# A 3x3 convolution as seven products of up to 128 rows from tiles of shifted channel blocks, and smaller tiles for data that comes back from DRAM

## The chip, the cores and the metric

The program runs on one core of a Trainium2 chip. The metric is the device time of one execution in microseconds, the median of several runs. A profile of one further execution goes with it; its times are in microseconds (us) from the start of the span.

## The reference

The input is 32 images of 56 x 56 positions and 96 channels, float32. Two layers follow one another:

```python
# layer 0, each image
h  = layernorm(x) over channels * ln_w + ln_b
x1 = (h @ w_in + b_in)[..., :192]            # the second half of w_in is not used
y  = conv3x3(x1, conv_w, 'SAME') + conv_b    # 192 -> 96 channels
x  = x + silu(y)
# layer 1, on the 3136 positions of an image
t  = x
h  = relu(bn1(layernorm(t) @ w1.T))          # 96 -> 192
X  = fft(h, axis=positions, norm='ortho')
xr = relu(X.real*rd - X.imag*idg + rb);  xi = relu(X.imag*rd + X.real*idg + ib)
t  = t + bn2(real(ifft(xr + 1j*xi)) @ w2.T)  # 192 -> 96
t  = t + qffn(layernorm(t))                  # 96 -> 384 -> 96, values rounded to 8-bit floats
```

## The kernel before

The two linear steps of layer 0 are folded at the start into one 3x3 convolution of 96 normalised channels plus a row of ones for the biases (`weff`, 97 rows, 9 taps). A Fourier transform of 3136 = 112 x 28 points is made of two stages of matmuls with tables.

One image is a tile `t` of 112 partitions x 28 x 96: partition p holds positions 28p to 28p+27. Work goes in seven groups of four columns j (`G4`, `NG`), in the spectrum in seven groups of four frequency pairs (`PG`, `NS`). These are the steps of an image b, with their engines and lines:

- `image`: the normalised input of group g is transposed on TensorE (L258, tile `tp_im`) and copied by VectorE (DVE) into `img` (L265), a zero-padded picture of 97 x 58 x 58, channels on partitions.
- `conv` (L273): nine products, one per tap, each reading `img` shifted by (dy, dx), into a PSUM tile `cv` of 96 x 448. ScalarE (ACT) takes it out with Silu (L275, tile `s`), TensorE transposes it back (L281) and DVE adds it to `t` (L283).
- `layernorm` (L241 to L248), on DVE, ACT and GpSimd (POOL), three times an image: `a` of the next input, `b` after the convolution, `c` after the attention part.
- `channels` and `transform_a` (L288 to L303): transposes, product with `w1`, Relu, first transform stage; the result `u` goes to DRAM as `da`, one DMA per group.
- `spectrum` (L305 to L369): `da` is loaded back into the tile `at` by seven DMAs (L312), into one large buffer. `forward(g, i)` multiplies with the table `fb_sb` (L320, tile `px`), and ACT, DVE and POOL form the rectified spectrum (L330 to L339). `inverse(g)` multiplies with `w2` (L347, `pg`), copies to `gw` on ACT (L349), multiplies with `ib_sb` (L352, `pe`), copies to `es` on DVE (L354), and sends `es` to DRAM as `de` (L355). Between the groups, `between(g)` makes `image` group g of the next image.
- `transform_out`: `de` comes back as `y` by seven DMAs (L368); the last transform stage `py` (L374) is added to `t` (L376), and LayerNorm `c` follows.
- `ffn_in`, `ffn_out` (L381 to L405): the FFN of image b runs interleaved with the convolution of image b+1, group by group.

All these DMAs are issued from one queue, SyncE's (SP). ACT's queue issues three loads at the start and nothing later. The order of instructions on each engine is fixed before the program runs, by a planner that takes the source's order as priority and lets ready work of later steps go ahead; so the transposes of `image` stand ahead of the first `px`, and the convolution of the next image begins before `py`. On the chip each engine then works strictly in that order.

Buffers named below: PSUM tags with two buffers each are `tp` (transposes), `a` (`cv`, `pf`, `pa`), `b` (`pg`, `pe`, `po`), `c` (`ph`, `px`, `py`). In SBUF, `es` has three buffers (pool `w3`), and `y` two, each for a whole image.

Of the kernel before, what the change touches and what calls it, by code (L numbers as in the profile page):

```python
# [32 lines left out]
F32 = mybir.dt.float32  # L36
F16 = mybir.dt.float16
F8 = mybir.dt.float8e5
AF = mybir.ActivationFunctionType
# [3 lines left out]
C = 96  # L43
# [5 lines left out]
PG = 4  # L49
NS = NP // PG  # L50
H = 192
FF = 384
G4 = 4
NG = N2 // G4
EPS = 1e-5
# [11 lines left out]
def first(p):  # L67

    return 2 * (2 * N2 * p + min(p, PG))
# [3 lines left out]
def hybrid_kernel(ctx: ExitStack, tc: tile.TileContext, x, par, w_in, conv_w, w1, w2, fw1, fb1, fw2, fb2, fa, fb, ib, ia, out):  # L73
# [19 lines left out]
    nc.sync.dma_start(par_sb, par)  # L93
    convb = par_sb[:, CONV_B : CONV_B + 1]

    weff = const.tile([C + 1, 9, C], F32, name="weff")
    w1a = const.tile([C + 1, H], F32, name="w1a")
    w2a = const.tile([C, 2, C], F32, name="w2a")
    w1q = const.tile([C, FF], F8, name="w1q")
# [2 lines left out]
    b2q = const.tile([N1, G4, C], F16, name="b2q")  # L102


    img = const.tile([C + 1, HW + 2, HW + 2], F32, name="img")
    n2ts = [const.tile([C + 1, G4, N1], F32, name=f"n2t{i}") for i in range(3)]
    ys = [const.tile([113, N2, C], F32, name=f"y{i}") for i in range(2)]
    scal = const.tile([C, 3, 2], F32, name="scal")

    tpool = ctx.enter_context(tc.tile_pool(name="tpool", bufs=2))  # L110

# [7 lines left out]
    with tc.tile_pool(name="setup", bufs=1) as sp, tc.tile_pool(  # L119
# [12 lines left out]
        for g in range(2):  # L132
            ps = spp.tile([128, 512], F32, tag="ps", name=f"ps_wt{g}")
            nc.tensor.matmul(ps[:C, : C + 1], win[:, g * C : (g + 1) * C], diag, start=True, stop=True)
            nc.vector.tensor_copy(wt[:, g, :], ps[:C, : C + 1])
            nc.vector.tensor_tensor(
                wt[:, g, C : C + 1], wt[:, g, C : C + 1], par_sb[:, B_IN + g : B_IN + g + 1], ALU.add
            )
        for k in range(9):
            ps = spp.tile([128, 512], F32, tag="ps", name=f"ps_we{k}")  # L140
            for g in range(2):
                nc.tensor.matmul(ps[: C + 1, :C], wt[:, g, :], cw[:, g, k, :], start=(g == 0), stop=(g == 1))
            nc.vector.tensor_copy(weff[:, k, :], ps[: C + 1, :C])

        def bn_fold(scale, bias, at, n):

# [30 lines left out]
            nc.vector.tensor_copy(w2a[:, g, :], ps[:C, :C])  # L177
        ps = spp.tile([128, 512], F32, tag="ps", name="ps_o2")
        nc.tensor.transpose(ps[:1, :C], o2, ident[:C, :C])
        row = sp.tile([1, N2, C], F32, name="row")  # L180
        for i in range(N2):
            nc.vector.tensor_copy(row[:, i, :], ps[:1, :C])
        for y in ys:
            nc.sync.dma_start(y[112:113], row)
# [28 lines left out]
            nc.vector.tensor_copy(b2q[:, i, :], b28)  # L213

        nc.gpsimd.memset(img, 0.0)
        nc.gpsimd.memset(img[C : C + 1, 1 : HW + 1, 1 : HW + 1], 1.0)
        for n2t in n2ts:
            nc.gpsimd.memset(n2t[C : C + 1], 1.0)
        nc.sync.dma_start(fb_sb, fb)
        nc.scalar.dma_start(ib_sb, ib)  # L220


    big = ctx.enter_context(tc.tile_pool(name="big", bufs=1))
    xnp = ctx.enter_context(tc.tile_pool(name="xnp", bufs=2))
    work = ctx.enter_context(tc.tile_pool(name="work", bufs=2))
    w3 = ctx.enter_context(tc.tile_pool(name="w3", bufs=3))
# [31 lines left out]
            nc.tensor.transpose(ps[:, j, :], xn[:, g * G4 + j, :], ident[:N1, :N1])  # L258
        return ps

    inside = img[:C, 1 : HW + 1, 1 : HW + 1].rearrange("c r (h j) -> c j r h", h=2)

    def image(xn, b, g):
        ps = to_channels(xn, g, f"im{b}")
        nc.vector.tensor_copy(inside[:, g * G4 : (g + 1) * G4], ps.rearrange("c j (r h) -> c j r h", h=2))  # L265

    def conv(b, g):

        ps = psum.tile([C, N1, G4], F32, tag="a", name=f"cv_{b}_{g}")
        for k in range(9):  # L270
            dy, dx = divmod(k, 3)
            seen = img[:, dy : dy + HW, dx : dx + HW].rearrange("c r (h j) -> c r h j", h=2)
            nc.tensor.matmul(ps, weff[:, k, :], seen[:, :, :, g * G4 : (g + 1) * G4], start=(k == 0), stop=(k == 8))  # L273
        s = work.tile([C, G4, N1], F32, tag="s", name=f"s_{b}_{g}")
        nc.scalar.activation(s, ps.rearrange("c p j -> c j p"), AF.Silu, bias=convb)  # L275
        return s

    def conv_add(s, t, b, g):
        pt = psum.tile([N1, G4, C], F32, tag="tp", name=f"st_{b}_{g}")
        for j in range(G4):  # L280
            nc.tensor.transpose(pt[:, j, :], s[:, j, :], ident[:C, :C])  # L281
        tg = t[:, g * G4 : (g + 1) * G4, :]
        nc.vector.tensor_tensor(tg, pt, tg, ALU.add)  # L283

# [20 lines left out]
    def spectrum(da, b, between):  # L305


        de = dram.tile([NP, 112, C], F32, tag="de", name=f"de_{b}")
        at = big.tile([112, NP, H], F32, tag="at", name=f"at_{b}")
        rows = da.rearrange("n (k p) c -> (n k) p c", p=NP)  # L310
        for g in range(NS):
            nc.sync.dma_start(at[:, g * PG : (g + 1) * PG, :], rows[:, g * PG : (g + 1) * PG, :])  # L312
        gt = {}

        def forward(g, i):
            w = width(g * PG)
            px = psum.tile([C, PG, 2, w], F32, tag="c", name=f"px_{b}_{g}_{i}")
            for j in range(PG):
                p = g * PG + j
                nc.tensor.matmul(  # L320
                    px[:, j], at[:, p, i * C : (i + 1) * C], fb_sb[:, first(p) : first(p + 1)], start=True, stop=True
                )
            if i == 0:
                gt[g] = w3.tile([C, 2, PG, 2, w], F32, tag="gt", name=f"gt_{b}_{g}")
# [16 lines left out]
        def inverse(g):  # L341
            k = 2 * width(g * PG)
            pg = psum.tile([k, PG, C], F32, tag="b", name=f"pg_{b}_{g}")
            for j in range(PG):
                for i in range(2):
                    lhs = gt[g][:, i, j].rearrange("c r k -> c (r k)")
                    nc.tensor.matmul(pg[:, j, :], lhs, w2a[:, i, :], start=(i == 0), stop=(i == 1))  # L347
            gw = work.tile([k, PG, C], F32, tag="gw", name=f"gw_{b}_{g}")
            nc.scalar.copy(gw, pg)  # L349
            pe = psum.tile([112, PG, C], F32, tag="b", name=f"pe_{b}_{g}")  # L350
            for j in range(PG):
                nc.tensor.matmul(pe[:, j, :], ib_sb[:k, g * PG + j, :], gw[:, j, :], start=True, stop=True)  # L352
            es = w3.tile([112, PG, C], F32, tag="es", name=f"es_{b}_{g}")
            nc.vector.tensor_copy(es, pe)  # L354
            nc.sync.dma_start(de[g * PG : (g + 1) * PG].rearrange("p m c -> m p c"), es)  # L355
            del gt[g]

        for g in range(NS + 1):
            if g < NS:
                forward(g, 0)  # L360
                forward(g, 1)
            between(g)
            if g >= 1:
                inverse(g - 1)
        yt = ys[b % 2]
        rows = de.rearrange("p (k n) c -> (p k) n c", n=N2)
        for g in range(NG):
            nc.sync.dma_start(yt[:112, g * G4 : (g + 1) * G4, :], rows[:, g * G4 : (g + 1) * G4, :])  # L368
        return yt  # L369

    def transform_out(yt, t, b, g):

        py = psum.tile([N1, G4, C], F32, tag="c", name=f"py_{b}_{g}")
        nc.tensor.matmul(py, ia_sb, yt[:, g * G4 : (g + 1) * G4, :], start=True, stop=True)  # L374
        tg = t[:, g * G4 : (g + 1) * G4, :]
        nc.vector.tensor_tensor(tg, py, tg, ALU.add)  # L376

# [32 lines left out]
    layernorm(t_next, xa, "a0")  # L410
    for g in range(NG):
        image(xa, 0, g)
    before = None
    for b in range(nb + 1):
        if b < nb:
# [31 lines left out]
            layernorm(t_next, xa, f"a{b + 1}")  # L447

        def between(g):
            if more and g < NG:  # L450
                image(xa, b + 1, g)

        yt = spectrum(da, b, between)
        xc = norm_tile(f"c{b}")
        for g in range(NG):
            transform_out(yt, t, b, g)
            layernorm(t, xc, f"c{b}", ended(g))
        before = xc, t, b

# [95 lines left out]
```

## Time and profile before

| quantity | value |
|---|---|
| median of three runs | 5408.46 us (5400.78 to 5417.65) |
| profiled execution | 5414.79 us outside, span 5413.0 us |
| granted clock of TensorE, mean | 0.89 |
| busy share of TensorE matmuls, DVE, ACT, POOL | 85%, 57%, 36%, 44% |
| `cv` products (L273) | 4032 instructions, 1794.5 us busy |
| DMA bytes, mean rate | 316.72 MB, 59 GB/s |

A float32 product is two instructions in the profile. Matmuls overlap in their pipeline, so the mean duration of one (595 ns for `cv`) is longer than the distance from one start to the next. In the lists of groups and of instructions in time, a line gives source line, engine, operation, output <- inputs, and in brackets the time for which the engine was idle before it and what ended that.

### The profile page before, as it was taken

The page shows a single profiled execution, that of the slowest core. Times are in us where ns is not written, and L with a number is a line of the kernel's source. Part 1 is how long each engine was busy: PE and PEld are TensorE (multiplying, and loading weights), DVE is VectorE, ACT ScalarE, POOL GpSimd, SP SyncE. Part 2 cuts the span into 40 slices and gives each one's busy share as a digit, 9 for nine tenths or more (in the row PEclk, how much of TensorE's full clock was granted, in tenths as well). Part 3 has the DMA queues.
Part 4 walks back from the last instruction along what each step waited for, and adds up shares of the span by engine and source line. Part 5 has one row for each costly group of instructions (what it writes and reads, how often), then busy time and mean ns, then how long its engine had stood idle before and what let it go on. Part 6 is the DMA issues. An engine that isn't in the chain of part 4 may idle for free. (4 is left out here: it accounts for less than half of the span.)

```text
span 5413.0 us, 65386 instructions
## 1 busy us (share of the span) xinstructions
PE 4589.3 (85%) x23123; PEld 2942.3 (54%) x23123; DVE 3073.5 (57%) x6540; ACT 1945.4 (36%) x3970; POOL 2379.5 (44%) x2062
## 2 busy tenths in 40 slices
PE   6888888888888888988888888889888898888886
PEld 3555555555455554555554555545555455555555
DVE  3555555555555555556555555555555556555555
ACT  1333333333333343333433333433334333333333
POOL 3443544444444444444444444444444444434443
PEclk9988898888988889988989888889888898888987
DMA  2122211222202222112222022221222211222112
GB/s 52 52 72 72 57 54 34 72 72 58 66 22 71 72 61 66 48 43 72 72 57 62 26 72 72 59 67 29 62 72 61 65 43 48 72 69 58 52 36 72
DMA packets 277376, 316.72 MB, mean 59 GB/s; under 512 B 118808, under 2 KB 244568, under 8 KB 269656
## 3 DMA queue, kind: packets, MB, share of 16 engines
q1 hardware_dynamic: 275170, 310.44, 20.4%
q8 instruction: 184, 3.01, 0.2%
q10 hardware_dynamic: 1880, 2.09, 0.1%
q14 instruction: 142, 1.16, 0.1%
HBM read 158.31 MB, written 154.14 MB: 58 GB/s over the span
## 5 line engine op out<-in xcount | busy, mean ns | idle before, releaser
L273 PE MATMUL cv<-img,weff 97*96 97x448 f32 x4032 | 1794.5, 595 | 4.6 <-ACT h L387 2.5
L273 PEld LDWEIGHTS cv<-img,weff 97*96 97x96 f32 x4032 | 664.9, 170 | 952.6 <-issue 903.3
L337 POOL TENSOR_SCALAR sv<-sv 96x224 f32<-96x224 f32 (+1 forms) x448 | 428.7, 957 | 890.6 <-DVE sv L335 890.6
L320 PE MATMUL px<-fb_sb,at 112*96 112x112 f32 (+1 forms) x3584 | 568.7, 309 | 84.9 <-issue 51.2
L347 PE MATMUL pg<-w2a,gt 96*112 96x96 f32 (+1 forms) x3584 | 523.5, 299 | 67.1 <-DVE gt L339 64.8
L320 PEld LDWEIGHTS px<-fb_sb,at 112*96 112x96 f32 x3584 | 487.6, 203 | 117.3 <-issue 89.8
L347 PEld LDWEIGHTS pg<-w2a,gt 96*112 96x112 f32 (+1 forms) x3584 | 473.2, 211 | 98.4 <-DVE gt L339 97.5
L275 ACT ACTIVATE s<-cv,par_sb 96x448 f32<-96x448 f32 x224 | 140.4, 627 | 1031.8 <-PE cv L273 1031.8
L330 ACT ACTIVATE av<-px,par_sb 96x224 f32<-96x224 f32 (+1 forms) x448 | 198.2, 442 | 808.7 <-PE px L320 729.6
L405 POOL TENSOR_TENSOR t<-t,y 112x384 f32<-112x384 f32 x224 | 212.8, 950 | 569.1 <-DVE y L403 569.1
L258 PE MATMUL tp_im<-ident,xn_a 112*96 112x112 f32 x896 | 183.9, 372 | 322.2 <-POOL xn_a L248 277.7
L389 DVE TENSOR_SCALAR h<-h,b1q 128x448 f16<-128x448 f16 x672 | 289.9, 454 | 273.6 <-ACT h L387 267.5
L243 POOL TENSOR_TENSOR xn_c<-t,mu_c 112x768 f32<-112x768 f32 (+1 forms) x128 | 167.4, 1308 | 590.6 <-DVE mu_c L242 587.2
L243 POOL TENSOR_TENSOR xn_a<-t,mu_a 112x768 f32<-112x768 f32 (+1 forms) x128 | 165.9, 1307 | 495.1 <-DVE mu_a L242 375.9
L387 ACT CAST h<-pf 128x448 f16<-128x448 f32 x672 | 344.1, 532 | 67.9 <-PE pf L385 65.7
L288 DVE COPY n2t<-tp_n 96x448 f32<-96x448 f32 x224 | 138.4, 618 | 380.9 <-PE tp_n L258 380.9
L301 PE MATMUL pa<-h,fa_sb 112*112 112x384 f32 x896 | 348.6, 510 | 2.4 <-ACT h L299 2.4
L381 DVE CAST n3t<-tp_n 96x448 fp8e5<-96x448 f32 x224 | 137.1, 613 | 372.9 <-PE tp_n L258 372.9
L297 PE MATMUL ph<-w1a,n2t 97*112 97x192 f32 x1792 | 341.1, 327 | 0.0
L258 PEld LDWEIGHTS tp_im<-ident,xn_a 112*96 112x96 f32 x896 | 137.0, 182 | 374.4 <-POOL xn_a L248 362.2
L247 POOL TENSOR_TENSOR var_b<-var_b,mhalf 112x8 f32<-112x8 f32 (+1 forms) x128 | 209.6, 1637 | 217.3 <-DVE var_b L246 215.0
L352 PE MATMUL pe<-gw,ib_sb 112*112 112x96 f32 (+1 forms) x1792 | 266.4, 302 | 42.0 <-ACT gw L349 41.5
(105 smaller groups left out, 7858.8 us busy)
## 6 DMA issues: line engine op xcount, KB each, us to landing
da<-u SPq DMA_DIRECT2D x224, 336.0 KB, 3.2
at<-da SPq DMA_DIRECT2D x224, 336.0 KB, 6.3
t<-in_x SPq DMA_DIRECT2D x32, 1176.0 KB, 7.7
de<-es SPq DMA_DIRECT2D x224, 168.0 KB, 2.3
y<-de SPq DMA_DIRECT2D x224, 168.0 KB, 3.3
out<-t SPq DMA_DIRECT2D x32, 1176.0 KB, 5.9
ib_sb<-in_ib ACTq DMA_DIRECT2D x1, 1396.5 KB
fb_sb<-in_fb SPq DMA_DIRECT2D x1, 1375.5 KB
```

What stands on the lines that cost most here:

```text
L243: nc.gpsimd.tensor_tensor(xc, t[:, j0:j1, :], mu.unsqueeze(2).to_broadcast([N1, n, C]), ALU.subtract)
L258: nc.tensor.transpose(ps[:, j, :], xn[:, g * G4 + j, :], ident[:N1, :N1])
L273: nc.tensor.matmul(ps, weff[:, k, :], seen[:, :, :, g * G4 : (g + 1) * G4], start=(k == 0), stop=(k == 8))
L297: nc.tensor.matmul(ph[:, j, :], n2t[:, 2 * j2 + j, :], w1a, start=True, stop=True)
L301: nc.tensor.matmul(pa, fa_sb, h, start=True, stop=True)
L320: nc.tensor.matmul(px[:, j], at[:, p, i * C : (i + 1) * C], fb_sb[:, first(p) : first(p + 1)], start=True, stop=True)
L337: nc.gpsimd.tensor_scalar(sv[:, 1], sv[:, 1], 0.0, -1.0, ALU.max, ALU.mult)
L347: nc.tensor.matmul(pg[:, j, :], lhs, w2a[:, i, :], start=(i == 0), stop=(i == 1))
L352: nc.tensor.matmul(pe[:, j, :], ib_sb[:k, g * PG + j, :], gw[:, j, :], start=True, stop=True)
L387: nc.scalar.copy(h1, pf)
L389: nc.vector.tensor_scalar(h2, h1, b1q[:, k : k + 1], 0.0, ALU.add, ALU.max)
L405: nc.gpsimd.tensor_tensor(tg, tg, y2, ALU.add)
```

## The change

- The convolution reads three tiles instead of `img`: `ta` and `tb` of 128 partitions and `tcc` of 105, each 56 x 58 positions. `ta` and `tb` hold four 32-channel blocks of the picture, each shifted by its own dx; the shift dy is made when reading, so each serves three products. `tcc` holds the last block (channels 64 to 95 at dx = 2) at three shifts dy, and nine rows of ones (one per tap, for the bias), and serves one product. That is seven products instead of nine.
- The three tiles are built once an image by `pack`: eleven DMAs of 32 partitions x 12,992 bytes from SBUF to SBUF, issued from ACT's queue. `pack` stands after `forward(4)` of the spectrum; to have the picture ready by then, `between` makes two groups of `image` at a time.
- The picture is stored with its two axes exchanged, so that the 56 rows r are contiguous: the DVE copy of `image` writes runs of 56, and the products read runs of 56 (before: runs of 4).
- The weights are arranged into seven tiles `wp` by 20 small DMAs at the start, and the rows of ones are put into `tcc` by nine.
- To make room: `at` becomes three buffers of one group each, loaded three groups ahead; `y` becomes four buffers of one group, loaded inside `transform_out`; `es` has two buffers instead of three (pool `work`).

```diff
-    weff = const.tile([C + 1, 9, C], F32, name="weff")
+    wp = const.tile([128, 7, C], F32, name="wp")
...
-    img = const.tile([C + 1, HW + 2, HW + 2], F32, name="img")
+    img = const.tile([C, P58 + 1, P58], F32, name="img")
+    ta = const.tile([128, HW, P58], F32, name="ta")
+    tb = const.tile([128, HW, P58], F32, name="tb")
+    tcc = const.tile([C + 9, HW, P58], F32, name="tcc")
-    ys = [const.tile([113, N2, C], F32, name=f"y{i}") for i in range(2)]
+    ys = [const.tile([113, G4, C], F32, name=f"y{i}") for i in range(4)]
...
+        for i, blocks in enumerate((BLOCKS_A, BLOCKS_B)):
+            for j, (c, dx) in enumerate(blocks):
+                nc.sync.dma_start(wp[32 * j : 32 * j + 32, 3 * i : 3 * i + 3, :], taps[32 * c : 32 * c + 32, dx])
+        for dy in range(3):
+            nc.sync.dma_start(wp[32 * dy : 32 * dy + 32, 6, :], taps[64:96, 2, dy])
+        for k in range(9):
+            nc.sync.dma_start(wp[C + k : C + k + 1, 6, :], weff[C : C + 1, k, :])
...
-        row = sp.tile([1, N2, C], F32, name="row")
-        for i in range(N2):
+        row = sp.tile([1, G4, C], F32, name="row")
+        for i in range(G4):
...
-        nc.vector.tensor_copy(inside[:, g * G4 : (g + 1) * G4], ps.rearrange("c j (r h) -> c j r h", h=2))
+        nc.vector.tensor_copy(inside[:, g * G4 : (g + 1) * G4], ps.rearrange("c j (r h) -> c j h r", h=2))
+
+    def pack():
+        src = flat(img)
+        for tile, blocks in ((ta, BLOCKS_A), (tb, BLOCKS_B)):
+            for j, (c, dx) in enumerate(blocks):
+                nc.scalar.dma_start(
+                    flat(tile)[32 * j : 32 * j + 32], src[32 * c : 32 * c + 32, dx * P58 : dx * P58 + FLAT]
+                )
+        for dy in range(3):
+            nc.scalar.dma_start(
+                flat(tcc)[32 * dy : 32 * dy + 32], src[64:96, 2 * P58 + dy : 2 * P58 + dy + FLAT]
+            )
...
-        for k in range(9):
-            dy, dx = divmod(k, 3)
-            seen = img[:, dy : dy + HW, dx : dx + HW].rearrange("c r (h j) -> c r h j", h=2)
-            nc.tensor.matmul(ps, weff[:, k, :], seen[:, :, :, g * G4 : (g + 1) * G4], start=(k == 0), stop=(k == 8))
+        for k in range(7):
+            tile, rows = ((ta, 128), (tb, 128), (tcc, C + 9))[k // 3]
+            seen = tile.rearrange("k (h j) r -> k h j r", h=2)[:, :, g * G4 : (g + 1) * G4, k % 3 : k % 3 + HW]
+            nc.tensor.matmul(ps, wp[:rows, k, :], seen, start=(k == 0), stop=(k == 6))
...
-        at = big.tile([112, NP, H], F32, tag="at", name=f"at_{b}")
-        for g in range(NS):
-            nc.sync.dma_start(at[:, g * PG : (g + 1) * PG, :], rows[:, g * PG : (g + 1) * PG, :])
+        def back(g):
+            ats[g] = w3.tile([112, PG, H], F32, tag="at", name=f"at_{b}_{g}")
+            nc.sync.dma_start(ats[g], rows[:, g * PG : (g + 1) * PG, :])
+        for g in range(3):
+            back(g)
...
-            es = w3.tile([112, PG, C], F32, tag="es", name=f"es_{b}_{g}")
+            es = work.tile([112, PG, C], F32, tag="es", name=f"es_{b}_{g}")
...
                 forward(g, 0)
                 forward(g, 1)
+            if g + 3 < NS:
+                back(g + 3)
             between(g)
...
+        y = ys[(b * NG + g) % len(ys)]
+        nc.sync.dma_start(y[:112], rows[:, g * G4 : (g + 1) * G4, :])
...
         def between(g):
-            if more and g < NG:
-                image(xa, b + 1, g)
+            if not more:
+                return
+            for i in (2 * g, 2 * g + 1):
+                if i < NG:
+                    image(xa, b + 1, i)
+            if 2 * g == NG + 1:
+                pack()
```

For image 0, `pack` is called once before the loop.

## The prediction, made before the changed kernel was run

> **What bounds the kernel now.** I read the page for busy shares, then the PE timeline of one image, then busy time by stretch, then the DMA issues. The images repeat exactly: the first product of a convolution starts at 2034.15 and again at 2197.97 us, so one image costs 163.8 us and 32 of them 5242 of the 5413 us. TensorE (PE) is busy 85%, but that is an average over stages. The stretches, one image in four parts (us, then busy us per engine, then the granted clock):
>
> ```profile
> 2034.00:2061.20 27.20, 21.57 (x70) 9.57 (x68) 14.49 (x24) 4.68 (x7) 11.41 (x8) 0.96 0.19 58
> 2061.20:2113.80 52.60, 52.14 (x217) 25.42 (x217) 26.06 (x59) 16.36 (x31) 26.34 (x23) 0.96 0.00 0
> 2156.00:2203.00 47.00, 41.22 (x297) 35.89 (x297) 32.25 (x80) 20.94 (x49) 13.99 (x15) 0.87 0.11 27
> ```
>
> Only the second, 52.6 us with five convolutions and the FFN of the image before, is bound by PE (52.14 busy; no other engine above 26.4). In the first, PE waits, as its timeline shows from the last spectrum group on:
>
> ```profile
> 2197.97 0.94 PE L273 MATMUL cv<-img,weff 97*96 97x448 f32 x2
> 2198.76 1.03 PE L352 MATMUL pe<-gw,ib_sb 112*112 112x96 f32 x8
> 2199.62 6.82 PE L273 MATMUL cv<-img,weff 97*96 97x448 f32 x16
> 2206.28 1.46 PE L374 MATMUL py<-y,ia_sb 113*112 113x384 f32 x4
> ...
> 2225.05 0.89 PE L281 MATMUL st<-ident,s 96*112 96x96 f32 x4 [5.64 <-ACT s L275]
> ```
>
> Convolution 0 fills the round trip of the spectrum through DRAM (`de` out, `y` back), which ends at 2206.28 with `py`; after it the LayerNorm of the attention result runs through DVE, POOL and ACT until 2225, PE idling 5.64 us at its end. Convolutions 0 and 1 lie beside those waits; 2 to 6 set time.
>
> **The products.** 4032 instructions are 224 convolutions of 9 products, two passes each. In the instruction records the starts lie 0.387 us apart for dx=0 and dx=2, and 0.465 for dx=1: a convolution takes 12 x 0.387 + 6 x 0.465 = 7.4, and 7.51 in the median. Both kinds move 448 columns; what differs is where runs of 4 numbers begin. The new reading has runs of 56 at a pitch of 58. The fast kind is the nearer row: 14 x 0.388 = 5.43, a gain of 2.08; were all 0.465, 6.51 and a gain of 1.0. Rows in use rise from 97 to 128; `pf` with 96 and `po` with 128 rows show no price for rows, so nothing for that. Five convolutions an image give 10.4; I take 10.0, since DVE (26 us of what becomes 42) starts to show. For 32 images, image 0 gaining a little more as it has no FFN beside it: 320 us.
>
> **What is added on ACT's queue.** `pack` issues 11 DMAs after forward(4), ahead of inverse(3)'s copy `gw` on ACT. It needs the image copy of group 6. Today that copy loses to all of the spectrum's DVE work (it runs at 2196.39); now its place is after forward(3), so near 2181.5, just before pack's. A DMA issue holds a queue 0.3 to 0.7 us (0.30 for `de`, 0.43 for `at`, 0.70 for `ib_sb` on ACT): 11 x 0.4 = 4.4 us, from 3.3 to 7.7. Queued behind them are `gw` and the `av` of forward(5):
>
> ```profile
> 2182.42 0.54 ACT L332 ACTIVATE av<-px,par_sb 96x224 f32<-96x224 f32 x1
> 2183.26 0.48 ACT L349 COPY gw<-pg 112x384 f32<-112x384 f32 x1 [0.30 <-PE pg L347]
> 2185.48 0.44 ACT L330 ACTIVATE av<-px,par_sb 96x224 f32<-96x224 f32 x1 [1.74 <-PE px L320]
> ```
>
> `gw` moves from 2183.3 to about 2187.4, then `pe`, PE's next `px`, and DVE; ACT has 1.5 us of slack in a group of 5 us, DVE half a step ahead. DVE is late by about 3.3. That is the least that the round trip moves.
>
> **The copies themselves.** 11 x 32 rows x 12,992 bytes are 4466 KB an image. No transfer of before goes from SBUF to SBUF at size. Nearest are the two with rows of 10.7 KB:
>
> ```profile
> t<-in_x SPq DMA_DIRECT2D x32, 1176.0 KB, 7.7
> de<-es SPq DMA_DIRECT2D x224, 168.0 KB, 2.3
> y<-de SPq DMA_DIRECT2D x224, 168.0 KB, 3.3
> out<-t SPq DMA_DIRECT2D x32, 1176.0 KB, 5.9
> ...
> f<-in_fw SPq DMA_DIRECT2D x2, 144.0 KB, 6.6
> win<-in_w_in SPq DMA_DIRECT2D x1, 72.0 KB, 22.2
> ```
>
> Less the 2.0 that even a tiny transfer takes (`y<-row`), 1176 KB take 3.9 (`out`) to 5.7 us (`t`); 3.80 times that is D = 14.8 to 21.7 us. Pack reads SBUF and writes it, so the slower of the two should weigh more, but `t` shares its queue with `da`: I take D = 19. First issue 2183.0, 1.9 to the first byte, so pack lands at P = 2184.9 + D = 2203.9. Convolution 0 starts today at 2198, needs `ta` for its first three products and the last copy only for its seventh, so that by itself costs a few us at most.
>
> The real cost lies with the small packets. `de` goes out as 448 packets of 384 bytes, 28 on each of 16 engines; pack is 22 packets of 13 KB on each. `win` shows what such a neighbour does: 72 KB took 22.2 us at the start, behind small packets that advanced one or two a microsecond, in the packet records, while ACT's queue moved `ib_sb` in packets of 12.5 KB. The queues take turns by the packet. So the `de` of group 3, out at about 2190, gets one packet through per packet of pack, and lands when pack does. The change also cuts the `es` buffers from 3 to 2: `es` of group 5 waits for that landing, on DVE, and behind it stand `pe` of group 6 (its PSUM buffer), `es` of group 6, its `de`, and all `y`. Today:
>
> ```profile
> 2197.19 0.54 DVE L354 COPY es<-pe 112x384 f32<-112x384 f32 x1
> 2199.82 0.56 DVE L354 COPY es<-pe 112x384 f32<-112x384 f32 x1 [2.09 <-PE pe L352]
> ```
>
> From the last `es` to `py` are 6.46 us (2199.82 to 2206.28). New: P + 0.5, `es` 0.55, `pe` 1.1, so the last `es` at P + 2.2 and `py` at P + 8.7 = 2193.6 + D; the round trip ends later by D - 12.7, or by ACT's 3.3 if that is more. D = 14.8: 3.3; D = 19: 6.3; D = 21.7: 9.0. All later stages of the image shift by it, and convolutions 0 and 1 fit into the longer wait.
>
> The Trainium skill speaks against these copies: its page "SBUF — State Buffer", section "Door 1: The DMA port swizzle", says that 32 or 64 neighbouring partitions reach only half of the 16 DMA ports. By its 435 GB/s for all ports, as an estimate, 4.57 MB through half of them would take 21 us; no run here shows it, and the sum above does without it.
>
> **Data back in smaller tiles.** `at` is now fetched three groups ahead. Group g+3 is asked for when group g's `px` end; three groups ahead are some 10 us against 6.3 to landing, and the last is out near 2179, before pack: nothing, 3 us if pack started earlier. The first of three lands no later than the first of seven. `y` comes in four buffers; the fifth load waits for the first `py`, 3.3 us for a need 3.9 us after it: nothing to 0.5, beside the LayerNorm. The image copy writes runs of 56 now; like `n2t` 618 against 952 ns, 2.3 us of DVE an image, in a stretch where PE waits for POOL: nothing.
>
> **Once, at the start.** Pack of image 0 has no cover: 1.9 + 19 = 21; 20 small weight DMAs 8; 24 row copies fewer -4; ones rows 2: 27 us.
>
> **Sum,** on the profiled execution (5414.8 outside, 5413.0 span): 5414.8 - 320 + 31 x 6.3 + 27 = 5317. It stands 6.3 above the median of the runs, so 5311.
>
> **The rivals.** *Pack hides.* D at the `out` rate or less, only ACT's issues cost: 5414.8 - 320 + 31 x 3.3 + 27 = 5224. If shorter convolutions also let convolution 2 into the 5.64 us wait for ACT's `s`, up to 5.0 an image more: 5069. For it: 42 us lie between the early image copies and convolution 0, and the order on the engines is not the source's. Against: copy 6 comes late.
>
> *Pack is the bound (slower).* One mechanism: the copies outlast the stretch from 2183 to the last `es`. It decides from 31 (D - 12.7) + 27 = 320, D = 22.2, barely above the `t` row. At twice `out`'s time, D = 29.6, as every byte crosses SBUF twice: 5414.8 - 320 + 524 + 27 = 5646. The DMA share then shows a solid block from 2185 to 2215, with PE idle after it.
>
> *The products get no faster each,* all at 0.465: gain 4.9 an image, 5414.8 - 157 + 195 + 27 = 5480. This is also the case in which the change does only part of what it says.
>
> **How the numbers follow.** Forecast 0.37 (its own range 5220 to 5400), pack hides 0.20, pack is the bound 0.33, products no faster 0.10. Within 0.3% (16 us, about what a measurement here can tell) lies only the upper edge of the forecast and a little of the slower rival: 0.05. Faster: 0.35 of the forecast, 0.20, and 0.02 of the rest, 0.57; slower 0.38. The range takes in half of the hiding case's gift and most of the slower case: 5110 to 5600, with 0.18 outside, two thirds of it above.
>
> **What would show it.** Line L273's successor: 3136 instructions, starts 0.388 apart. On ACT, a block of 11 issues of some 4 us in mid-spectrum. `de` landing over 10 us in the groups beside pack, against 2.3. The last `es` near 2206 on the old scale, `py` near 2213. The PE-bound stretch about 42.5 us instead of 52.6. I am wrong if `de` lands in 2 to 4 us beside pack, if pack's landing is under 15 or over 25 us, if the first packs stand elsewhere than after forward(4), or if DVE's waits fill the shortened stretch.

## The result, and the profile after

The changed kernel is slower: 5667.78 us in the median of four runs (5662.41 to 5672.28) against 5404.62 of before (5396.65 to 5417.65), a ratio of 1.0484 with a 95% interval of [1.046, 1.0508]. The prediction, 5311 us and faster, is wrong in sign, and the time lies above its range of 5110 to 5600 us. The profiled execution has a span of 5660.5 us (5413.0 before).

The page's busy times and its groups first; columns of a group: busy us, mean ns of one | idle us before, what ended most of it.

```profile
PE 4263.9 (75%) x22227; PEld 2819.6 (50%) x22227; DVE 3046.9 (54%) x6516; ACT 1944.2 (34%) x3970; POOL 2403.8 (42%) x2063
...
L312 PE MATMUL cv<-ta,wp 128*96 128x448 f32 x1344 | 682.2, 656 | 267.1 <-DMA ta<-img 190.2
...
L392 ACT COPY gw<-pg 112x384 f32<-112x384 f32 (+1 forms) x224 | 107.4, 479 | 809.3 <-DMA tcc<-img 560.4
```

TensorE is busy 75% where it was 85%, so time went into waiting, not into work. The third line says where to look first: `gw`, the copy that follows `pack` on ACT's queue, waited 560.4 us in all in waits that the profile puts down to the copies, 30 times, 19.4 us at the longest.

Busy time by stretch for one image (us; PE, PEld, DVE, ACT, POOL busy with counts; granted clock, DMA share, GB/s): the spectrum from its first `px` to its last `es`; 16 us out of its middle; from the first `py` to convolution 2; convolutions 2 to 6.

```profile
2076.40:2140.60 64.20, 50.77 (x320) 39.59 (x318) 31.45 (x80) 22.21 (x51) 14.11 (x15) 0.83 0.48 110
2106.00:2122.00 16.00, 7.99 (x20) 3.48 (x20) 1.45 (x4) 0.00 (x0) 0.96 (x1) 0.68 0.99 216
2146.20:2166.30 20.10, 11.84 (x30) 5.87 (x30) 14.45 (x23) 4.08 (x7) 11.42 (x8) 0.58 0.13 38
2166.30:2204.60 38.30, 37.55 (x163) 18.98 (x164) 24.01 (x52) 12.73 (x24) 22.97 (x20) 0.96 0.00 1
```

The stretch that is bound by TensorE has shrunk to 38.3 us, as wanted. In the second line ACT does nothing for 16 us, while the DMA engines are full at 216 GB/s. The timeline of ACT shows why (start, duration, queue or engine; in brackets idle time and what ended it):

```profile
2102.89 0.52 ACTq L298 DMA_DIRECT2D ta<-img  x1
2103.22 0.54 ACT L375 ACTIVATE av<-px,par_sb 96x224 f32<-96x224 f32 x1
2103.44 5.08 ACTq L298 DMA_DIRECT2D ta<-img  x3
2108.57 7.95 ACTq L298 DMA_DIRECT2D tb<-img  x4
2116.56 6.23 ACTq L302 DMA_DIRECT2D tcc<-img  x3
2122.83 0.48 ACT L392 COPY gw<-pg 112x384 f32<-112x384 f32 x1 [19.07 <-DMA tcc<-img]
```

The first issue takes 0.52 us; from `tb` on one takes 2.0 (7.95 for four, 6.23 for three). A copy is 32 rows of 12,992 bytes, 416 kB; at 216 GB/s that is 1.92 us. So in this row the queue takes the next copy about as fast as the bytes of earlier ones leave, and ACT stands at the issues for 19.9 us. DVE's next line waits with it:

```profile
2124.53 0.45 DVE L377 SCALAR_TENSOR_TENSOR sv<-px,par_sb,av 96x224 f32<-96x224 f32 x1 [16.71 <-ACT av L375]
```

On TensorE, products of the next image's convolutions 0 and 1 stand ahead of `pe` in that time, and the round trip at the end is as before:

```profile
2106.80 0.98 PE L363 MATMUL px<-fb_sb,at 112*96 112x112 f32 x8 [1.32 <-DVE sv L379]
2113.87 7.01 PE L312 MATMUL cv<-ta,wp 128*96 128x448 f32 x12 [6.09 <-DMA ta<-img]
2122.05 4.72 PE L312 MATMUL cv<-tb,wp 128*96 128x448 f32 x12 [1.17 <-DMA tb<-img]
2126.61 0.94 PE L395 MATMUL pe<-gw,ib_sb 112*112 112x96 f32 x8
...
2146.16 7.31 PE L417 MATMUL py<-y,ia_sb 113*112 113x384 f32 x12 [5.59 <-DMA y<-de]
```

DMA issues (KB each, median us from issue to landing):

```profile
ta<-img ACTq DMA_DIRECT2D x128, 406.0 KB, 7.0
tb<-img ACTq DMA_DIRECT2D x128, 406.0 KB, 7.3
tcc<-img ACTq DMA_DIRECT2D x96, 406.0 KB, 7.5
...
de<-es SPq DMA_DIRECT2D x224, 168.0 KB, 2.3
y<-de SPq DMA_DIRECT2D x224, 168.0 KB, 2.5
```

`de` still lands in 2.3 us in the median. Only group 2's goes out as `pack` begins, and it lands in 4.8 us; those of groups 3 to 6 go out after `pack` has landed (here at 2128.17 and later, the last packet of `pack` ends at 2127.40). The starvation that the forecast rests on isn't there.

An image by stages, worked out from the traces as means over images 2 to 29 (us), for before, after, and the kernels of the experiments that the argument needs:

| stage | before | after | e1_sp | e8_last | e13_ports | e15_ports_last | e4_spread | e6_spread_last | e14_de_act |
|---|---|---|---|---|---|---|---|---|---|
| first `py` to convolution 2 | 21.4 | 20.1 | 18.8 | 14.9 | 20.1 | 14.8 | 20.1 | 18.7 | 16.0 |
| convolutions 2 to 6 | 47.8 | 38.4 | 38.4 | 42.2 | 38.4 | 42.6 | 38.5 | 38.7 | 42.4 |
| to the first `ph` | 5.4 | 7.7 | 7.9 | 7.9 | 7.7 | 7.8 | 8.0 | 8.0 | 8.1 |
| first `px` to last `es` | 46.8 | 63.6 | 52.2 | 63.6 | 63.0 | 61.2 | 55.6 | 50.4 | 46.6 |
| last `es` to first `py` | 6.7 | 5.4 | 5.8 | 6.3 | 5.5 | 6.3 | 5.4 | 6.8 | 8.9 |
| whole image | 166.6 | 174.3 | 162.3 | 173.8 | 174.1 | 171.7 | 166.7 | 161.6 | 161.2 |

The two stages from the first `ph` to the first `px`, 38.6 to 39.4 us in all of them, are left out. The stages before the first `ph` fall from 74.6 to 66.2, a gain of 8.4; the spectrum and its round trip rise from 53.5 to 69.0, a loss of 15.5. Over all images the distance from one first `py` to the next rises by 7.35 in the mean; 31 times that, and 19.3 us more up to the first `py` of all (206.9 to 226.3), are 247 of the 247.5 us between the spans.

The mean granted clock of TensorE falls as well, from 0.89 to 0.836. That is not what makes the kernel slower than before: e1_sp (0.855) and e16_ports_sp (0.849), both described below, run at hardly more and are faster than before.

### The profile page after: what moved, and what is told of

Same layout as the page of the kernel before. It is cut to its first block, busy times and chain, and to the rows that moved or that the text cites. A ratio compares the mean times of both kernels' runs of the same rounds, so it can differ in the third digit from the quotient of the medians.

```text
span 5660.5 us, 64071 instructions
## 1 busy us (share of the span) xinstructions
PE 4263.9 (75%) x22227; PEld 2819.6 (50%) x22227; DVE 3046.9 (54%) x6516; ACT 1944.2 (34%) x3970; POOL 2403.8 (42%) x2063
## 3 DMA queue, kind: packets, MB, share of 16 engines
q1 hardware_dynamic: 276562, 310.77, 19.4%
## 4 chain that ended last, share of the span: by engine, by line
PE 30%; POOL 15%; DVE 14%; DMA 12%; ACTq 5%; issue 4%; ACT 3%; POOLq 0%; SPq 0%; DVEq 0%
PE cv L312 12%; ACTq L298 4%; PE px L363 4%; DMA t<-in_x 3%; DMA tb<-img 3%; PE pg L390 3%; POOL sv L380 3%; DMA out<-t 3%; POOL var_a L273 2%; PE pe L395 2%; POOL xn_a L274 2%; POOL xn_c L269 2%; POOL var_c L273 2%; PE pf L428 2%; PE po L440 2%
## 5 line engine op out<-in xcount | busy, mean ns | idle before, releaser
L312 PE MATMUL cv<-ta,wp 128*96 128x448 f32 x1344 | 682.2, 656 | 267.1 <-DMA ta<-img 190.2
L312 PE MATMUL cv<-tb,wp 128*96 128x448 f32 x1344 | 544.1, 544 | 41.8 <-DMA tb<-img 36.4
L312 PEld LDWEIGHTS cv<-ta,wp 128*96 128x96 f32 x1344 | 247.4, 197 | 604.0 <-issue 459.1
L377 DVE SCALAR_TENSOR_TENSOR sv<-px,par_sb,av 96x224 f32<-96x224 f32 (+1 forms) x448 | 198.0, 442 | 555.7 <-ACT av L375 553.7
L390 PE MATMUL pg<-w2a,gt 96*112 96x96 f32 (+1 forms) x3584 | 466.1, 279 | 34.0 <-DVE gt L382 29.5
L390 PEld LDWEIGHTS pg<-w2a,gt 96*112 96x112 f32 (+1 forms) x3584 | 421.5, 192 | 82.1 <-DVE gt L382 77.5
L312 PEld LDWEIGHTS cv<-tb,wp 128*96 128x96 f32 x1344 | 219.7, 165 | 348.3 <-issue 336.7
L417 PE MATMUL py<-y,ia_sb 113*112 113x384 f32 x448 | 241.2, 692 | 195.4 <-DMA y<-de 175.3
L392 ACT COPY gw<-pg 112x384 f32<-112x384 f32 (+1 forms) x224 | 107.4, 479 | 809.3 <-DMA tcc<-img 560.4
L270 ACT ACTIVATE sq_c<-xn_c 112x768 f32<-112x768 f32 (+1 forms) x128 | 97.6, 763 | 718.9 <-POOL xn_c L269 718.9
```

Of the source, the lines that this page charges most:

```text
L312: nc.tensor.matmul(ps, wp[:rows, k, :], seen, start=(k == 0), stop=(k == 6))
L417: nc.tensor.matmul(py, ia_sb, y, start=True, stop=True)
```

## The experiments

Theory A: ACT, held at the issues of `pack`, is the loss. Rivals: the bytes themselves (DMA bandwidth, `de` starving beside `pack`), TensorE's order (convolution products that wait for copies, ahead of `pe`), and the smaller tiles. All ratios below are to the kernel before, with 95% intervals.

**e1_sp**, the same copies from SP's queue:

```diff
-                nc.scalar.dma_start(      # twice, in pack()
+                nc.sync.dma_start(
```

> Pack's eleven copies go out from SP's queue instead of ACT's; nothing else differs from the changed kernel (174.2 us an image, 5668 us). Theory A (ACT stands still for some 19 us an image because its queue takes the next copy only when an earlier one has moved its bytes, and the copy gw and the av stand behind it): ACT and DVE go on; what is held now is SP, so the de of groups 3 and later wait behind pack and es of group 5 waits for its buffer, 9 to 14 us less an image than now, 5230 to 5390 us. Rival B (TensorE's own order: the products on ta and tb of two convolutions stand ahead of pe and pg and wait for pack): no gain, 5620 to 5690 us. Rival C (small packets of de crawl beside pack's large ones): 5400 to 5600 us, with de landing in over 10 us.

Measured: 5289.9 us, 0.9765 [0.9728, 0.9802]. One word in two places takes some 380 us off, with the same bytes and packets (13 KB packets take 1.012 us in the median in both). That is theory A's number and speaks against bandwidth as the cause. The order on TensorE moved as well, however: the 24 instructions of convolutions 0 and 1 that stood ahead of the `pe` of group 3 now stand behind the last `pe`. So this run alone doesn't tell ACT's hold from that order; e8_last does. The spectrum is still 5.4 us longer than before's. The waits of DVE name what replaced the hold (us in all, times, longest):

```profile
DVE es L397 <- DMA de<-es: 344.0, 32, 11.7
```

By the packet records, the `de` of groups 3 and 4 land 19.7 and 15.9 us after their `es` here (1.9 before), since `pack` stands ahead of them in SP's queue. This is the wait that the prediction foresaw, but through the queue's order.

**e2_order**, copies from ACT, alternating between channels 0 to 63 and 64 to 95:

```diff
...
+        for i in (0, 6, 1, 7, 2, 8, 3, 9, 4, 10, 5):
...
+            nc.scalar.dma_start(flat(tile)[to : to + 32], src[at : at + 32, by : by + FLAT])
```

> The same eleven copies from ACT's queue in another order: copies that read channels 0 to 63 and copies that read channels 64 to 95 take turns. If the 2.02 us of one copy is set by the half of the partitions that it reads and writes (packets of 13 KB take 1.01 us in the changed kernel, 0.49 at best), neighbours now use different halves and one copy takes 1.0 to 1.5 us; by theory A ACT is then held 11 to 15 us instead of 20 and the time falls by 5 to 9 us an image, to 5390 to 5510 us. If the 2.02 us is each DMA engine's own rate or SBUF to SBUF in general, nothing moves: 5640 to 5690 us. Rival B gives the same gain as A here.

Measured: 5636.8, 1.0418 [1.0394, 1.0442]; the packets' median falls from 1.012 to 0.959 us only, and from the first issue to the last landing are 24.1 us in the median against 25.0. ACT's block of issues does fall, from 19.9 to 14.7 us in the median (an issue takes 1.0 to 1.8 us from the fourth on), yet the spectrum is 64.1 us. TensorE's order takes the gain: in one image `gw` is done at 2118.41, but `pe` starts only at 2127.76, behind products of `ta` that waited 11.15 us for their copies, which now come spread over the row.

**e3_ta**, only the four `ta` copies after the first image (later images read old data in `tb` and `tcc`):

```diff
-    def pack():
+    def pack(whole=False):     # True for the first image alone; without it only ta
...
```

> After image 0 only the four copies into ta are made (tb and tcc keep image 0's data, so seven of the eleven copies are left out). Theory A: the first four issues of the changed kernel took 0.5 us or little more each, only later ones 2.0, so ACT is held 2 to 4 us and nearly all of the 20.8 us an image comes back: 5060 to 5180 us. Rival B: the products on ta still stand ahead of pe and wait for the four copies, some 8 us after the first issue: 5250 to 5350 us. Rival C: a third of the bytes, a third of the loss: 5200 to 5260 us.

Measured: 5211.75, 0.9631 [0.9607, 0.9655]. Four issues hold ACT little, and most of the loss is gone; the time is still 30 to 150 us above what A expected, mostly because A's 20.8 us lead an image down to 153.4 us, which is 163.8 - 10.4, while an image of before takes 166.6 in the mean. An image costs 159.5 us here, 7.1 less than before. That is net of the 2.1 us by which the spectrum is still longer (48.9 against 46.8), with a block of four issues of 5.6 us on ACT.

**e4_spread**, one copy per half group from ACT, and all image groups ahead of the first inverse:

```diff
-            if 2 * g == NG + 1:
-                pack()
...
+        def half(i):                 # called after each forward(g, 0) and (g, 1)
+            if more and 2 <= i < 13:
+                pack_moves()(i - 2)
```

> All seven groups of the picture are made at the spectrum's first step, and the eleven copies are issued from ACT's queue one after each half step of forward, from group 1 on (2.25 us or more apart, so that the one before has moved its bytes). All else as in the changed kernel. Theory A: each issue costs ACT 0.5 to 0.6 us and never waits; the spectrum is 2 to 6 us longer than before the change, and an image takes 155 to 160 us: 5080 to 5230 us. Rival B: the products wait for pack only if it lands after 2198 on the scale of before; it starts 15 us earlier, so the gain is the same unless the order puts the products earlier too: 5080 to 5400 us. Rival C (small packets crawl beside large ones): de of all groups lands in over 10 us instead of 2.3, es waits for its two buffers, 5300 to 5600 us.

Measured: 5434.2, 1.005 [1.0029, 1.007], well above A's 5080 to 5230. Each issue now takes 0.51 us, with no wait for the queue, and the spectrum falls from 63.6 to 55.6. `de` lands in 2.3 to 6.9 us (medians by group), so rival C's 10 us isn't there. What is left shows on DVE and TensorE:

```profile
2026.85 0.56 DVE L400 COPY es<-pe 112x384 f32<-112x384 f32 x1 [3.34 <-PE pe L398]
```

```profile
2021.34 3.92 PE L315 MATMUL cv<-ta,wp 128*96 128x448 f32 x10
2025.10 0.93 PE L366 MATMUL px<-fb_sb,at 112*96 112x112 f32 x8
2025.87 0.94 PE L398 MATMUL pe<-gw,ib_sb 112*112 112x96 f32 x8
```

Convolution products run between two groups, and `pe` stands behind them. So TensorE's order costs something once ACT is free. The next runs separate the two.

**e8_last**, the changed kernel with the product of `tcc` first in each convolution, so that no product is ready before the last copy lands:

```diff
-        for k in range(7):
+        for k in (6, 0, 1, 2, 3, 4, 5):
...
```

> The changed kernel with only the order of the seven products of a convolution altered: the product on tcc, whose copies pack issues last, comes first. With that TensorE's fixed order no longer holds products on ta and tb ahead of the pe and pg of groups 3 to 6; all convolution products stand after pg of group 5. ACT's queue is as before this edit. Theory A (ACT held by pack's issues for 19 us): the spectrum stays 14 to 17 us longer than before the change, 5600 to 5700 us. Rival B (TensorE's order: products wait for pack ahead of pe and pg): the spectrum comes back to 47 to 50 us and the time to 5150 to 5250 us.

Measured: 5654.8, 1.0434 [1.0413, 1.0456]; the spectrum stays at 63.6:

```profile
ACT gw L392 <- DMA tcc<-img: 571.3, 30, 19.2
```

The order of TensorE costs the spectrum nothing while ACT is held as long as this. With that order out of the way in both, the spectrum is 11.4 us longer here, with ACT held, than in e1_sp.

**e5_es3**, e1_sp with three `es` buffers instead of two:

```diff
-            es = work.tile([112, PG, C], F32, tag="es", name=f"es_{b}_{g}")
+            es = w3.tile([112, PG, C], F32, tag="es", name=f"es_{b}_{g}")
...
```

> Pack from SP's queue as in the run that took 5290 us, and es with three buffers again (y gives one up, three instead of four, for the room). In that run DVE waited 344 us in all, 11 us an image, for a de to land before it could write es, and the spectrum was 52.2 us against 46.8 before the change. If the two es buffers are the cause, the spectrum falls to 47 to 48 us: 5090 to 5180 us. If the last de is late anyway because it stands behind pack on the one queue, the wait only moves to py: 5250 to 5300 us.

Measured: 5338.15, 0.985 [0.9826, 0.9873]: a miss, no better than e1_sp and rather worse. DVE still waits 332.4 us for `de`: the next `es` now waits for the `de` of group 3, which is just as late. One more buffer doesn't help against a landing some 20 us off. Whether the buffer that `y` gave up makes it worse than e1_sp was not tried.

**e11_sp_spread**, copies spread over half groups on SP, with `tcc` first:

```diff
...
+            nc.sync.dma_start(flat(tile)[to : to + 32], src[at : at + 32, by : by + FLAT])
...
```

> Copies one by one after the half steps of forward, as in the spread run (5434 us), but from SP's queue, and the product on tcc first so that no convolution product stands inside the spectrum in TensorE's order. In the spread run the spectrum took 55.6 us, with DVE waiting three times 3.3 us for pe behind ten or twelve products on ta or tb. If that order was the cause of those 8.8 us, the spectrum is 47 to 49 us and the convolutions 0 and 1 stand beside the wait for y again: 5080 to 5180 us. If the cause is that large and small packets share the DMA engines, 5300 to 5450 us remain.

Measured: 5646.0, 1.0409 [1.0376, 1.0442], a miss on the other side. In TensorE's timeline the two halves of the last groups' `px` stand together behind `pe`, so forward and inverse no longer overlap: the last two take 13 us each, earlier ones 5 to 7. The products there are slower too (`pe` 1.81 us for eight, against 1.02 at 2278 us), at a granted clock of 0.50 from 2294 to 2303 us:

```profile
2294.11 1.81 PE L398 MATMUL pe<-gw,ib_sb 112*112 112x96 f32 x8 [0.62 <-ACT gw L395]
2295.72 3.19 PE L366 MATMUL px<-fb_sb,at 112*96 112x112 f32 x16
2301.22 0.69 PE L393 MATMUL pg<-w2a,gt 96*112 96x96 f32 x2 [2.31 <-DVE gt L385]
```

In the order planned for SP, `at` loads stand behind copies, and their `px` come late on TensorE. Moving a DMA to another queue also moved the order of TensorE.

**e9_tiles**, the kernel before with only the smaller tiles:

```diff
-    ys = [const.tile([113, N2, C], F32, name=f"y{i}") for i in range(2)]
+    ys = [const.tile([113, G4, C], F32, name=f"y{i}") for i in range(4)]
...
+            ats[g] = w3.tile([112, PG, H], F32, tag="at", name=f"at_{b}_{g}")
+            nc.sync.dma_start(ats[g], rows[:, g * PG : (g + 1) * PG, :])
```

> The kernel before with only the second part of the change: at in three buffers of a group, y in four buffers of a group, es in two, the convolution as it was. The prediction put this part at nothing: 5390 to 5425 us. Rival: the later requests of at and y cost a wait each image, 1 to 3 us: 5440 to 5510 us.

Measured: 5413.1, 0.9985 [0.9973, 0.9997]. That part of the change costs nothing.

**e6_spread_last**, the edits of e4_spread and e8_last together:

```diff
-            if 2 * g == NG + 1:
-                pack()
...
+                pack_moves()(i - 2)
...
+        for k in (6, 0, 1, 2, 3, 4, 5):
...
```

> Both edits of two earlier runs together: one copy for each half group, issued from ScalarE (as in the spread kernel, 5434), and the products that read tcc first in each convolution, so that TensorE's order no longer holds the convolution's ta and tb products inside the spectrum. Theory: what was left over of the spread kernel's loss (55.6 us from the first px to the last es against 46.8 before, three VectorE waits of 3.3 us on pe) is TensorE's order, in which convolution products wait for copies. Then that stretch falls to 47 to 50 us and the time to 5434 - 32 x (5.6 to 8.6) = 5160 to 5255, below both kernels. Rival: the loss is the copies themselves (eleven issues of 0.51 us on ScalarE, packets beside the groups' transfers), whatever TensorE's order: the stretch stays at 54 to 56 and the time at 5400 to 5440.

Measured: 5291.5, 0.9772 [0.9751, 0.9793]: the spectrum falls from 55.6 to 50.4, so about 5 of the 8.8 us that e4_spread had left were TensorE's order. The expectation is missed by 37 us; DVE still waits for `pe` 173 times, 1.9 us each, and whether that is ACT's issues was not tried.

**e13_ports**, the changed kernel with each copy taking every third channel to every fourth row (third in `tcc`), weights in the same order:

```diff
-                    flat(tile)[32 * j : 32 * j + 32], src[32 * c : 32 * c + 32, dx * P58 : dx * P58 + FLAT]
+                    flat(tile)[j:128:4], src[c:C:3, dx * P58 : dx * P58 + FLAT]
...
```

> The changed kernel with the same eleven copies of 406 KB from ScalarE, but each moves every third channel of img to every fourth row of ta and tb (every third of tcc), the weights' rows in the same new order, so that no copy lies on 32 neighbouring partitions. Theory: a packet of 13 KB takes 1.01 us in the changed kernel, against 0.49 at best, because 32 neighbouring partitions share half of the ways into SBUF; the source now lies two thirds on partitions 0 to 63 and the goal on all 128. Then a packet takes 0.5 to 0.7 us, an issue of a queue that is full 1.0 to 1.4 us in place of 2.02, ScalarE is held some 11 to 15 us in place of 20, and the time falls by 32 x (5 to 9) to 5380 to 5510. Rival: the 1.01 us is the DMA engines' own pace for so long a packet between two places of SBUF, whichever partitions they are: packets stay at 0.95 to 1.02 us and the time at 5640 to 5670.

Measured: 5654.06, 1.0439 [1.0421, 1.0458]. The packets did in part what the theory says: 0.664 us in the median instead of 1.012, a quarter of them at 0.486, but a quarter above 0.92, so that the mean falls only from 0.981 to 0.775. The hold falls less than expected, from 19.9 to 17.4 us in the median and not to 11 to 15, the time hardly:

```profile
2106.79 6.34 ACTq L298 DMA_DIRECT2D tb<-img  x4
2113.17 4.97 ACTq L302 DMA_DIRECT2D tcc<-img  x3
2118.18 0.48 ACT L392 COPY gw<-pg 112x384 f32<-112x384 f32 x1 [16.77 <-DMA tb<-img]
```

```profile
2119.55 4.72 PE L312 MATMUL cv<-tb,wp 128*96 128x448 f32 x12 [0.83 <-DMA tb<-img]
2124.11 0.94 PE L395 MATMUL pe<-gw,ib_sb 112*112 112x96 f32 x8
```

`gw` is done at 2118.66, `pe` starts at 2124.11: the products of `tb` stand between them. ACT's gain was taken by TensorE's order, as in e2_order.

**e15_ports_last**, e13_ports with `tcc` first:

```diff
-        for k in range(7):
+        for k in (6, 0, 1, 2, 3, 4, 5):
...
```

> The kernel with the copies on every third channel and fourth row (5654) with the products that read tcc first in each convolution, so that no cv<-ta or cv<-tb product stands ahead of pe in TensorE's queue. Theory: ScalarE's hold and TensorE's order cover each other. In the changed kernel taking away the order alone gave nothing, since ScalarE was held longer; with the hold down from 19.4 to some 16.4 us, pe then came late by cv<-tb products (VectorE's es waited 4.75 us for pe). With both edits the stretch from the first px to the last es falls by the 3.0 us of the shorter hold, to 60 to 61, and the time to 5560 to 5590. Rival: the hold's length does not price the loss and something else holds the groups: 5640 to 5665.

Measured: 5578.81, 1.0297 [1.0274, 1.0319], inside the theory's 5560 to 5590, with the spectrum at 61.2. Alone, each edit took 0.5% of before's time off (1.0484 to 1.0434 and to 1.0439), together 1.9%. The two waits cover each other, and with the order out of the way the length of ACT's hold prices the loss. In the three kernels that issue a row of copies from ACT and have no product of `ta` or `tb` ahead of the first `pe` held, the spectrum is longer than before's by 2.1 us for a hold of 5.6 (e3_ta), 14.4 for 17.5 (this run) and 16.8 for 19.9 (e8_last, holds in the median): 3 to 3.5 us less than the hold each time.

**e14_de_act**, e1_sp with `de` issued from ACT:

```diff
-            nc.sync.dma_start(de[g * PG : (g + 1) * PG].rearrange("p m c -> m p c"), es)
+            nc.scalar.dma_start(de[g * PG : (g + 1) * PG].rearrange("p m c -> m p c"), es)
```

> The kernel with pack on SP's queue (5290) with one more word changed: de<-es is issued from ScalarE in place of SyncE, so that it does not stand behind pack's copies in one queue. Theory: the 5.4 us that this kernel's stretch from the first px to the last es is still longer than before's (52.2 against 46.8) are the groups whose es waits for a de that stands behind 406 KB copies on the same queue (VectorE waits 344 us in all there). Then these waits fall below 60 us in all, the stretch to 47 to 49 us, and the time to 5290 - 32 x (3 to 5) = 5130 to 5195, with up to 60 us more if the seven issues of ScalarE for each image (about 0.4 us each) stand in the chain: 5130 to 5250. Rival: de's packets are slow beside pack's whatever queue they stand in, or pack's issue holds another transfer on SP: the stretch stays at 51 to 53 and the time at 5270 to 5310.

Measured: 5253.31, 0.9693 [0.9673, 0.9713]. The spectrum falls to 46.6, no longer than before's, and DVE's wait for `de` is gone from its list: the queue it stood in was the cause. The time lies just above the range; the stretch to `py` has grown to 8.9. By the packet records `de` lands 2.0 to 5.9 us after `es` (medians by group), with `pack`'s packets on the other queue.

**e16_ports_sp**, e14_de_act with the copies of e13_ports:

```diff
-                    flat(tile)[32 * j : 32 * j + 32], src[32 * c : 32 * c + 32, dx * P58 : dx * P58 + FLAT]
+                    flat(tile)[j:128:4], src[c:C:3, dx * P58 : dx * P58 + FLAT]
...
```

> The kernel with pack on SP's queue and de on ScalarE's (5253) with the copies on every third channel and every fourth row. Theory: its stretch from the last es to the first py is 8.9 us, against 5.8 with de on SP, because y's loads stand behind pack's last copies in SP's queue (the first y load is issued at 2147.92, 3.7 us after the last de). With packets at half the time pack is through some 4 to 5 us sooner, that stretch falls to 5 to 6.5, and the time by 32 x (2.5 to 4) to 5125 to 5175. Rival: the groups, not the copies, set when SP's queue comes to y's loads: 5235 to 5260.

Measured: 5237.12, 0.9666 [0.9652, 0.9681], the fastest but for e3_ta, but by 16 us (the intervals overlap) and not by 80 to 130: the theory failed, and the time is the rival's. The stretch to `py` stays at 8.9 though `pack` is issued by 2132.3, long before the last `de` at 2137.78. TensorE's timeline names what stands there:

```profile
2135.78 1.37 PE L395 MATMUL pe<-gw,ib_sb 112*112 112x96 f32 x8
2136.99 3.92 PE L312 MATMUL cv<-ta,wp 128*96 128x448 f32 x10
2140.75 4.67 PE L312 MATMUL cv<-tb,wp 128*96 128x448 f32 x12
2145.26 0.92 PE L312 MATMUL cv<-tcc,wp 105*96 105x448 f32 x2
2146.02 1.46 PE L417 MATMUL py<-y,ia_sb 113*112 113x384 f32 x4
```

It is convolutions 0 and 1, ahead of `py`. Their time isn't won back behind it: convolution 2 comes sooner after the first `py` (16.0 us instead of 18.8 in e1_sp), but convolutions 2 to 6 then take 42.3 us instead of 38.4, so that from the first `py` to the end of the convolutions are 58.3 us, against 57.2 in e1_sp. What holds convolutions 2 to 6 there was not tried.

## Why the prediction was wrong

**The products: right, the term a little too large.** 3136 instructions, starts 0.376 us apart against the 0.388 taken, a convolution from its first to its last start 4.97 us in the median against 7.12. The stretch of convolutions 2 to 6 lost 9.4 against 10.0 forecast, but 2.3 came back behind it, where the LayerNorm `b` ends later than the products: 7.1 net; together with 1.3 ahead of convolution 2, 8.4. e3_ta, with few copies, gains 7.1 for the whole image, its spectrum's loss of 2.1 included. The rival "no faster each" is refuted.

**ACT's queue: the step that failed.** The prediction priced 11 issues at 0.4 us from rows whose queues were not full, 4.4 us in all and 3.3 for DVE. The rows gave what an issue costs on an empty queue, and e4_spread confirms that price (0.51). In a row of eleven it is 2.0, the time in which the bytes of one copy move, and the block is 19.9 us. So the data's time, which the prediction put beside all other work, stood on ACT's own path. The round trip moved by 15.5 us and not by 6.3. Four runs together show that the hold is the cause: with TensorE's order out of the way and the hold left as it was, the spectrum stays at 63.6 (e8_last); with a shorter hold it falls by the difference (e15_ports_last, e3_ta); with the same bytes on another queue it is 52.2 (e1_sp). TensorE's order is a second wait, mostly covered by the first: 5.2 us once the copies are spread (e4_spread against e6_spread_last).

**The copies' own time: mis-sized.** From the first packet of `pack` to the end of its last are 23.5 us in the median, of which the 22 packets on each engine, at a mean of 0.981 us, are 21.6; taken were 19, with bounds of 14.8 to 21.7. The 1.9 us to the first byte, for which the prediction gives no row, were 1.2. By the prediction's own formula D = 23.5 would have given 5414.8 - 320 + 31 x 10.8 + 27 = 5457, still some 205 below the profiled execution: the loss lies not in the size of D, but in where it stands. The estimate that the prediction worked out from the Trainium skill's page "SBUF — State Buffer", section "Door 1: The DMA port swizzle", 21 us, lies near the 21.6. In e13_ports, which leaves the neighbouring partitions, the mean packet falls to 0.775 us, in the direction of that rule; but with copies of both halves taking turns (e2_order) it stays at 0.952, so what sets a packet's time is in part open.

**`de` starving by turns: wrong.** In the changed kernel ACT's hold kept `gw` back, so that no `es` was made while `pack` ran, and the `de` of groups 3 to 6 landed in 2.3 us; that of group 2, out just as `pack` began, took 4.8. Where they do run side by side on two queues (e14_de_act), the slowest group's `de` takes 5.9 us in the median, not the twenty-odd of one packet for one: while its 28 packets pass on an engine, 2 to 3 of `pack`'s do. A wait as long as the one forecast, 19.7 us, appears only where both share one queue (e1_sp).

**The tiles: right** (e9_tiles). **The start:** the first product of all comes 21.0 us later (65.6 to 86.7), against 27.

**The length of an image: misread.** The images don't repeat exactly. From one first `py` to the next are 163.0 to 168.9 us over images 2 to 29 of the kernel before, 166.6 in the mean; the prediction's 163.8 is one of the short ones. Its sum doesn't use that number, but the expectation of e3_ta does.

**The rivals.** "Pack is the bound" had the nearest number, 5646, and D is past the 22.2 from which it was to decide, but its mechanism isn't there: the copies do not outlast the stretch to the last `es`, which comes 13.2 us after their last packet in the median. The nearness of the number is luck. "Pack hides" has a number, 5224, near the 5253 and 5237 of e14_de_act and e16_ports_sp, but not its condition: there the copies are not faster but on another queue, and an image gains 5.4 to 6.1 us and not 6.7.

## What to carry to other kernels

In this kernel a row of large DMA issues on a compute engine's queue cost issue time alone only for the first two (0.52 and 0.60 us); from then on each took about 2.0 us, the time in which the bytes of one copy move, and the engine's next compute instruction waited. So price a row of large copies on a compute engine by their bytes, put them on a queue whose engine computes nothing, and then ask which small, urgent transfer now stands behind them on that queue. Where one wait covers another, removing either shows almost nothing: e8_last and e13_ports gave 0.5% each, and both together 1.9%.

## What the runs showed of the hardware that was not expected

An issue of a 416 kB copy took 0.51 us where one was issued per half group, and 2.0 us in a row of eleven (1.0 to 1.8 where copies from two parts of the channels took turns, e2_order, though the eleven landed hardly sooner). Copies on 32 neighbouring partitions moved in packets of 1.01 us (13 KB) in the median, interleaved ones in 0.664, but the issuing of all eleven only went from 19.9 to 17.4 us. Packets of 384 bytes on one queue passed packets of 13 KB on another with a landing of 2 to 6 us, not one for one (e14_de_act).
